# Inverse roots of twenty norms: from ScalarE's square root to bit operations and Newton steps on VectorE, in a two-layer MetaFormer kernel on Trainium2

## The chip, the cores and the metric

The kernel runs on one core of a Trainium2 chip. The metric is the device time of one execution in microseconds (us); a profile of one execution comes beside it. A core has a matrix engine (PE, with its weight loads counted apart as PEld), VectorE (DVE), ScalarE (ACT), GpSimd (POOL) and a queue engine (SP), which run their own instruction streams in order and wait for one another through semaphores.

## The reference

The input is `x`, four images of 384 channels and 32 x 32 positions, in fp32. There are two layers, and each has two residual steps, a mixing one and a feed-forward one, with a norm over the channels of one position ahead of each.

```python
def _ln_c(v, eps=1e-6):            # over the channels of a position
    m = jnp.mean(v, axis=1, keepdims=True)
    s = jnp.var(v, axis=1, keepdims=True)
    return (v - m) / jnp.sqrt(s + eps)
...
# --- layer 0 (metaformer) ---
x = x + _L0_conv_ref(_ln_c(x), ...)        # attention with relative tables, then w_proj
t = _to_tokens(x)
t = t + _L0_ffn_ref(_ln_t(t), ...)         # 384 -> 1536, exact Gelu, -> 384, weights are Kronecker products
x = _from_tokens(t, x)
# --- layer 1 (metaformer) ---
x = x + _L1_conv_ref(_ln_c(x), ...)        # sum of depthwise convolutions, folded into one of 7 x 7
t = _to_tokens(x)
t = t + _L1_ffn_ref(_ln_t(t), ...)         # softmax gate, top 2 of 4 experts, exact Gelu
x = _from_tokens(t, x)
```

`_ln_t` is the same over the last axis, with `eps=1e-5`. Four norms are taken of each image, then: one ahead of attention, and three behind it.

## The kernel before

The program has three phases. `qkv_phase` takes the first norm and makes queries, keys and values; `attention_phase` runs until about 1507 us; `rest_phase` does all the rest, and the change is in it alone.

In `rest_phase` an image is a tile `xb` of 128 partitions x 3 channel chunks x 1024 positions, worked on in two halves of 512 positions (`TOK`). The steps of an image b are these:

- `project` (L971): nine matmuls of a half (`proj_ps`), VectorE's addition of bias and residual (L980), and the statistics for the first norm behind attention.
- `net` (L988): the feed-forward of layer 0. The inverse root is spread over the partitions by `to_partitions` (L110): VectorE multiplies it into a diagonal (`s_dg`, L115) and PE multiplies ones with it (`all_ps`, L117). Twelve Gelus on ScalarE (`hs` from `f_ps`, L1022) stand between two sets of matmuls; VectorE adds the result to `xb` (L1030).
- `normalise` (L1051): statistics of the second norm, mean and inverse root each through `to_partitions`, then VectorE subtracts the mean (`xc`, L1061).
- `image` (L1065): VectorE multiplies by the scale into a padded image `img`. `convolve` (L1079): bias (L1084) and then 49 taps of three chunks, each one VectorE instruction of 128 x 1024 (L1089); in image 0 a part of the taps is done on PE by diagonal matmuls (`tap_ps`, `taps_ps`).
- `gates` (L1184): logits by PE (`gate_ps`, L661), statistics of the third norm (eight groups of 128 positions), `g_shift`, then `gate_weights` (L679) with a softmax, whose exponential is ScalarE's (L694), and the top two. The ranks of the chosen follow on PE (`before_ps`, L755) and VectorE.
- `scatter` (L1223): GpSimd writes the normalised rows to their slots in HBM.
- `blocks` (L1244): the experts, in blocks of 128 rows that are gathered again (`xg`), transposed (`xT_ps`), multiplied with weights that GpSimd fetches (`e_ps`, L1301), put through Gelu on ScalarE with a bias (`eh`, L1304) and multiplied again (`y_ps`, L1279). Four groups have 13, 16, 16 and 22 blocks; a block has twelve steps. `combine` adds the experts' results to `xb` at the end.

All three norms take their statistics in `token_stats` (L78): PE transposes 128 positions (`row_ps`, L87), VectorE takes mean and variance (`s_st`, `s_mv`, L89 and L90), and at the end ScalarE takes the root of the variance plus `eps` (L96) and VectorE its reciprocal (L97). It is called twice an image by `project`, twice by `normalise`, with 128 x 4 values each, and once by `gates` with 128 x 8 values: twenty calls. `row_ps`, `proj_ps`, `f_ps` and `e_ps` share the three PSUM banks of the pool `ps_h`.

The order of each engine's instructions comes from two places. The program interleaves generators: `blocks` calls `more` after every step of an expert block, and `more` (L1475) advances the work of the coming images (`others`, L1407) for as long as a clock of estimated costs says so; `convolve` yields such a cost per tap. The numbers that `token_stats` and the others yield are those estimates. Below that, a list scheduler with modelled times sets each engine's order; instructions that pass through `pin` or `keep_in_program_order` (the taps of images 0 and 1, and a one-column `memset` after each tap of images 1 to 3, L1097) keep theirs. The compiler puts a table load ahead of each activation on ScalarE whose function is not in the table that is loaded. Root, Gelu and Exp alternate behind attention.

Of the kernel before, what the change touches and what calls it, by code (L numbers as in the profile page):

```python
# [11 lines left out]
F32 = mybir.dt.float32  # L12
AF = mybir.ActivationFunctionType
ALU = mybir.AluOpType
# [4 lines left out]
P = 128  # L19
# [33 lines left out]
NOT_LAST = (2 * (B - 1) * N + NEXP * (BLK - 1)) // BLK - sum(COUNTS[:-1])  # L53
MAXB = B * N // BLK
OUTSIDE = 1e6


PACKS = [
# [12 lines left out]
def bcast(ap, dim, n):  # L71

    dims = [list(d) for d in ap.ap]
    dims[dim] = [0, n]
    return bass.AP(ap.tensor, ap.offset, dims)


def token_stats(nc, pools, ident, x, eps, rows=None, step=4):  # L78


    small, psum, tag = pools
    nj = x.shape[2] // P
    mv = small.tile([P, nj, 2], F32, tag=f"s_mv{nj}", name="s_mv")
    for j in range(nj):
        ps = psum.tile([P, TOK], F32, tag=tag, name="row_ps")
        for k in range(KC):
            nc.tensor.transpose(ps[:, k * P : (k + 1) * P], x[:, k, j * P : (j + 1) * P], ident)  # L87
        st = small.tile([P, 6], F32, tag="s_st", name="s_st")
        nc.vector.bn_stats(st, ps[:, :C])  # L89
        nc.vector.bn_aggr(mv[:, j, :], st)  # L90
        if rows is not None:
            nc.scalar.copy(rows[j], ps[:, :C])
        if j % step == step - 1:
            yield 0.7 * step, 0.45 * step
    rstd = small.tile([P, nj, 1], F32, tag=f"s_rstd{nj}", name="s_rstd")
    nc.scalar.activation(rstd, mv[:, :, 1:2], AF.Sqrt, bias=eps)  # L96
    nc.vector.reciprocal(rstd, rstd)  # L97
    return mv[:, :, 0:1], rstd
# [11 lines left out]
def to_partitions(nc, pools, ident, one, values):  # L110

    small, psum, tag = pools
    nj = values.shape[1]
    dg = small.tile([P, nj, P], F32, tag="s_dg", name="s_dg", bufs=1)
    nc.vector.tensor_tensor(dg, bcast(ident.unsqueeze(1), 1, nj), bcast(values, 2, P), ALU.mult)  # L115
    ps = psum.tile([P, TOK], F32, tag=tag, name="all_ps")
    nc.tensor.matmul(ps, one, dg.rearrange("p j n -> p (j n)"), start=True, stop=True)  # L117
    return ps
# [535 lines left out]
def gate_logits(nc, pools, ident, gw, x, logits):  # L654


    psum, hid = pools
    ps = psum.tile([P, TOK], F32, tag="m", name="gate_ps")
    for k in range(KC):
        for h in range(N // TOK):  # L660
            nc.tensor.matmul(  # L661
                ps[32 * h : 32 * h + 32, :], gw[:, k, :], x[:, k, h * TOK : (h + 1) * TOK],
                start=(k == 0), stop=(k == KC - 1),
            )
    lgs = []
    for h in range(N // TOK):
        lg = hid.tile([P, TOK], F32, tag="hs", name="logits", bufs=HS)
        nc.scalar.copy(lg[:32], ps[32 * h : 32 * h + 32])
        lgs.append(lg)
    yield 0.1, 3.0  # L670
    for j in range(N // P):
        n0 = j % (TOK // P) * P
        nc.tensor.transpose(
            logits[:, 32 * j : 32 * j + 32], lgs[j // (TOK // P)][:32, n0 : n0 + P], ident[:32, :32]
        )
    yield 0.1, 1.5
# [140 lines left out]
def block_list(nc, small, cst, group, parts, done):  # L817
# [51 lines left out]
    nc.vector.tensor_tensor(over, ks, bcast(turned[:, :, m:], 1, nb), ALU.is_ge)  # L869
    nc.vector.scalar_tensor_tensor(where, over, OUTSIDE, where, ALU.mult, ALU.add)  # L870
    nc.vector.tensor_scalar(where, where, slot[:, 0:1], cst["wrow"][:, 0:1], ALU.add, ALU.add)
# [9 lines left out]
    nc.vector.tensor_tensor(held[:, :2], expert[:, :2, :], group["before"], ALU.is_equal)  # L881
    nc.vector.scalar_tensor_tensor(row, bcast(held, 2, 2), OUTSIDE, row, ALU.mult, ALU.add)
    nc.vector.tensor_copy(group["row"], row)
# [10 lines left out]
def rest_phase(tc, cst, x, ao_d, ins, xs_d, y_d, x2_d, out):  # L894
# [7 lines left out]
    nc = tc.nc  # L902
    ident, one = cst["ident"], cst["one"]
    with ExitStack() as es:
# [5 lines left out]
        small = es.enter_context(tc.tile_pool(name="r_small", bufs=2))  # L910
# [3 lines left out]
        stp = (small, ps_h, "h")  # L914
# [56 lines left out]
        def project(xs, at):  # L971

            if True:
                for m in range(KC):
                    ps = ps_h.tile([P, TOK], F32, tag="h", name="proj_ps")
                    for k in range(KC):
                        nc.tensor.matmul(  # L977
                            ps, wproj[:, k, m * P : (m + 1) * P], at[:, k, :], start=(k == 0), stop=(k == KC - 1)
                        )
                    nc.vector.scalar_tensor_tensor(  # L980
                        xs[:, m, :], ps, bproj[:, m : m + 1], xs[:, m, :], ALU.add, ALU.add
                    )
                    yield 0.7, 2.7

                _, rstd = yield from token_stats(nc, stp, ident, xs, cst["eps5"])
                return rstd

        def net(b, xs, rstd):  # L988
# [62 lines left out]
        def normalise(xb, halves, which=range(2)):  # L1051

            for half in which:
                xs = xb[:, :, half * TOK : (half + 1) * TOK]
                mean, rstd = yield from token_stats(nc, stp, ident, xs, cst["eps6"])
                mps = to_partitions(nc, (small, ps_m, "m"), ident, one, mean)
                sps = to_partitions(nc, (small, ps_m, "m"), ident, one, rstd)
                scale_sb = work.tile([P, TOK], F32, tag="scale", name="scale")
                nc.scalar.copy(scale_sb, sps)
                xc = work.tile([P, KC, TOK], F32, tag="xc", name="xc")  # L1060
                nc.vector.tensor_tensor(xc, xs, bcast(mps.unsqueeze(1), 1, KC), ALU.subtract)  # L1061
                halves.append((xc, scale_sb))
                yield 3.0, 2.0
# [120 lines left out]
        def gates(b):  # L1184

            xb, im = xbs[b], images[b]
            rows = [new_row() for _ in range(nj)]
            logits = ps_m.tile([P, TOK], F32, tag="m", name="logits_ps")
            yield from gate_logits(nc, (ps_m, hid), ident, gw, xb, logits)
            mean, rstd = yield from token_stats(nc, stp, ident, xb, cst["eps5"], rows, 2)  # L1190
            shift = small.tile([P, nj, 1], F32, tag="g_shift", name="g_shift")
            nc.vector.scalar_tensor_tensor(shift, mean, -1.0, rstd, ALU.mult, ALU.mult)
            yield from gate_weights(nc, small, logits, gb, rstd, im["mask"], im["top"])
            for j, row in enumerate(rows):
                nc.scalar.activation(row, row, AF.Identity, bias=shift[:, j, :], scale=rstd[:, j, :])
                im["rows"].append(row)
                if b and j % 2:
                    yield 1.0, 0.0
            yield 0.0, 0.0

        def new_row():
            return hid.tile([P, C], F32, tag="rows", name="rows", bufs=16)
# [181 lines left out]
        def ahead(b, halves):  # L1384
            if b < B:
                yield from enter(b)
                yield from normalise(xbs[b], halves)
# [107 lines left out]
@with_exitstack  # L1495
def metaformer_kernel(ctx: ExitStack, tc: tile.TileContext, ins, out):
    nc = tc.nc
    cp = ctx.enter_context(tc.tile_pool(name="const", bufs=1))
    dram = ctx.enter_context(tc.tile_pool(name="scratch", bufs=1, space=DRAM))
    ident = cp.tile([P, P], F32, name="ident")  # L1500
    make_identity(nc, ident)
    one = cp.tile([P, P], F32, name="one")
    nc.vector.memset(one, 1.0)
    cst = {"ident": ident, "one": one}
    for name, v in (("eps5", 1e-5), ("eps6", 1e-6)):
        t = cp.tile([P, 1], F32, name=name)
        nc.vector.memset(t, v)
        cst[name] = t
    qk_d = dram.tile([2 * C, NT], F32, name="qk_d")
    v_d = dram.tile([HEADS, P, B * NBLK * VW], F32, name="v_d")  # L1510
    ao_d = [dram.tile([C, B, YT * IMG], F32, name=f"ao_d{i}") for i in range(2)]
    x2_d = dram.tile([C, NT], F32, name="x2_d")
    xs_d = dram.tile([NEXP * CAP, C], F32, name="xs_d")
    y_d = dram.tile([ALL * BLK, C], F32, name="y_d")

    with tc.tile_pool(name="held", bufs=1) as pool:
        held = [
            pool.tile([64 + HD, *n], F32, name=name)
            for name, n in (("kq", [NT]), ("kk", [B, N // 2]), ("tab", [SPAN, ZW]))
        ]  # L1520
        qkv_phase(tc, cst, ins["x"], ins["w_qkv"], qk_d, v_d, xs_d)
        attention_phase(tc, cst, held, ins["tabs"], ins["tv"], qk_d, v_d, ao_d, list(range(HEADS)))
    rest_phase(tc, cst, ins["x"], ao_d, ins, xs_d, y_d, x2_d, out)
# [71 lines left out]
```

## Time and profile before

| what | value |
|---|---|
| runs | 3082.57, 3087.72, 3088.3 us; median 3087.72 |
| the profiled execution | 3092.57 us, span 3090.6 us, TensorE clock 0.976 |
| `attention_phase` ends, about | 1507 us |
| image 0: first convolution tap | 1592.2 us |
| gate of image 0, 1, 3: statistics ready | 1747.05, 2003.04, 2506.63 us |
| last norm done, experts of the last groups and the sum left | from about 2530 us |
| VectorE: taps of 128 x 1024 (L1089) behind 1500 us | 490, mean 1277 ns |
| VectorE: diagonal of the inverse root (L115) | 16, mean 729 ns |
| VectorE: reciprocal of 128 x 4 (L97) behind 1500 us | 16, mean 172 ns |

A line of groups names the code line, the engine, the operation, output and inputs by the program's names, then the count, busy time, mean duration, and the idle time of the engine just ahead with what ended it. In a line of waits, `PE all_ps L117 <- DVE s_dg L115` means that PE stood before `all_ps` until VectorE had finished `s_dg`. Times are counted from the first instruction of the profiled execution.

### The profile page before, as it was taken

The page shows a single profiled execution, that of the slowest core. Times are in us where ns is not written, and L with a number is a line of the kernel's source. Part 1 is how long each engine was busy: PE and PEld are TensorE (multiplying, and loading weights), DVE is VectorE, ACT ScalarE, POOL GpSimd, SP SyncE. Part 2 cuts the span into 40 slices and gives each one's busy share as a digit, 9 for nine tenths or more (in the row PEclk, how much of TensorE's full clock was granted, in tenths as well). Part 3 has the DMA queues.
Part 4 walks back from the last instruction along what each step waited for, and adds up shares of the span by engine and source line. Part 5 has one row for each costly group of instructions (what it writes and reads, how often), then busy time and mean ns, then how long its engine had stood idle before and what let it go on. Part 6 is the DMA issues. An engine that isn't in the chain of part 4 may idle for free.

```text
span 3090.6 us, 63376 instructions
## 1 busy us (share of the span) xinstructions
PE 2929.9 (95%) x25391; PEld 2020.6 (65%) x25391; DVE 1956.6 (63%) x3575; ACT 1370.8 (44%) x2833; POOL 1170.7 (38%) x1132
## 2 busy tenths in 40 slices
PE   8997999999999999999899789999999989999996
PEld 4544676777677677776533347776577867777775
DVE  2226787878787877777568869999899640001101
ACT  1104666666767666666322232333342243233332
POOL 3223747473747473737400122252124231124412
PEclk9998999999999999999999879999999999999998
DMA  3796565656565656564500314734243065366742
GB/s 123 259 320 212 130 203 131 206 132 203 134 202 134 200 131 196 136 199 128 186 21 34 128 31 156 274 136 154 75 175 132 26 229 215 134 227 250 263 180 72
DMA packets 262791, 500.55 MB, mean 162 GB/s; under 512 B 134736, under 2 KB 186832, under 8 KB 254816
## 3 DMA queue, kind: packets, MB, share of 16 engines
q1 hardware_dynamic: 169168, 247.12, 26.0%
q0 software_dynamic: 43424, 227.84, 20.0%
q10 hardware_dynamic: 49904, 21.53, 3.6%
q8 instruction: 200, 3.28, 0.5%
q14 instruction: 95, 0.78, 0.1%
HBM read 543.58 MB, written 152.37 MB: 225 GB/s over the span
## 4 chain that ended last, share of the span: by engine, by line
PE 67%; DVE 13%; issue 11%; POOL 4%; DMA 3%; ACT 2%; another core or an unknown queue 0%; SPq 0%; POOLq 0%; DVEq 0%; ACTq 0%
PE e_ps L1301 12%; PE y_ps L1279 12%; DVE xb L1089 8%; PE t_ps L410 7%; PE av_ps L227 7%; PE sc_ps L227 7%; PE tabq_ps L227 5%; PE a_ps L420 3%; PE tv_ps L227 2%; PE proj_ps L977 2%; PE tabk_ps L227 1%; PE tap_ps L1137 1%; DVE extra L402 1%; PE f_ps L1012 1%; PE o_ps L1016 1%
## 5 line engine op out<-in xcount | busy, mean ns | idle before, releaser
L1301 PEld LDWEIGHTS e_ps<-xT,w 128*128 128x128 f32 x4824 | 656.5, 193 | 217.7 <-issue 14.6
L353 POOL TENSOR_TENSOR bias<-b,s 128x416 f32<-128x416 f32 (+24 forms) x656 | 659.2, 1042 | 178.1 <-DMA s<-sd 157.5
L1301 PE MATMUL e_ps<-xT,w 128*128 128x128 f32 x4824 | 670.6, 277 | 14.1 <-DVE xb L1030 5.0
L1279 PE MATMUL y_ps<-w,eh 128*128 128x384 f32 x1608 | 651.9, 490 | 17.2 <-ACT eh L1304 14.8
L1089 DVE SCALAR_TENSOR_TENSOR xb<-img,pack,xb 128x1024 f32<-128x1024 f32 (+1 forms) x539 | 634.7, 1241 | 0.0
L1304 ACT ACTIVATE eh<-e_ps,w 128x128 f32<-128x128 f32 x804 | 292.9, 367 | 725.3 <-PE e_ps L1301 669.5
L1269 POOL DMA_INDIRECT w<-in_w,row x134 | 171.4, 1279 | 749.7 <-PE y_ps L1279 301.4
L402 DVE TENSOR_REDUCE extra<-arow 128x32 f32<-128x32 f32 (+24 forms) x768 | 381.3, 555 | 9.4 <-ACT arow L391 5.7
L381 DVE CUSTOM_DVE_ANT_0 arow<-sc_ps,bias 128x1024 f32<-128x1024 f32 x256 | 312.5, 1221 | 107.1 <-issue 55.5
L410 PEld LDWEIGHTS t_ps<-ident,arow 128*128 128x128 f32 x2048 | 221.2, 142 | 175.9 <-ACT aT L411 100.6
L391 ACT ACTIVATE arow<-arow,nm 128x1024 f32<-128x1024 f32 x256 | 302.4, 1181 | 70.8 <-DVE nm L381 70.8
L411 ACT COPY aT<-t_ps 128x512 f32<-128x512 f32 x512 | 278.6, 603 | 95.3 <-PE t_ps L410 95.0
L410 PE MATMUL t_ps<-ident,arow 128*128 128x128 f32 x2048 | 283.2, 282 | 17.1 <-ACT arow L391 17.0
L1282 DVE TENSOR_TENSOR yo<-y_ps,w 128x384 f32<-128x384 f32 x67 | 37.0, 553 | 396.0 <-PE y_ps L1279 387.8
L227 PE MATMUL sc_ps<-kk,qs 48*32 48x512 f32 x4096 | 279.2, 608 | 7.7 <-DVE nm L381 6.7
L1279 PEld LDWEIGHTS y_ps<-w,eh 128*128 128x128 f32 x1608 | 248.3, 193 | 31.9 <-ACT eh L1304 19.4
L227 PEld LDWEIGHTS av_ps<-aT,vb 128*64 128x64 f32 x4096 | 222.3, 137 | 52.0 <-ACT aT L411 40.4
L227 PE MATMUL av_ps<-aT,vb 128*64 128x128 f32 x4096 | 237.7, 274 | 0.0
L318 DVE STREAM_TRANSPOSE b<-tabk_ps 128x480 f32<-128x480 f32 x256 | 218.4, 983 | 23.5 <-PE tabk_ps L227 22.2
L227 PE MATMUL tabk_ps<-tab,kq 48*128 48x480 f32 x512 | 223.0, 582 | 6.1 <-DVE b L318 6.1
L227 PE MATMUL tabq_ps<-tab,kq 48*128 48x480 f32 x512 | 220.1, 579 | 2.1 <-ACT aT L411 1.4
L322 ACT COPY st<-tabq_ps 128x480 f32<-128x480 f32 x256 | 142.3, 560 | 71.0 <-PE tabk_ps L227 45.0
(211 smaller groups left out, 3163.4 us busy)
## 6 DMA issues: line engine op xcount, KB each, us to landing
sd<-st SPq DMA_DIRECT2D x128, 480.0 KB
s<-sd SPq DMA_DIRECT2D x256, 240.0 KB
xs_d<-zero POOLq DMA_DIRECT2D x8, 3072.0 KB
tvw<-in_tv SPq DMA_DIRECT2D x120, 192.0 KB
y_d<-yo SPq DMA_DIRECT2D x67, 192.0 KB
qk_d<-qk_sb POOLq DMA_DIRECT2D x48, 256.0 KB
qs<-qk_d SPq DMA_DIRECT2D x256, 48.0 KB
kq<-qk_d ACTq DMA_DIRECT2D x56, 192.0 KB
```

The costliest lines, as they stand in the source:

```text
L227: ins = nc.tensor.matmul(*args, **kw)
L318: turn = nc.vector.transpose(b2.rearrange("p e y x -> p x (e y)")[:, i + j], ps[:, j, : SPAN * IMG])
L353: nc.gpsimd.tensor_tensor(bias[:, y0:y1, :], bass.AP(b2.tensor, b2.offset + (e * IMG + y0) * IMG, [list(b2.ap[0]), [(step * IMG + 1) * IMG ...
L381: nc.vector.tensor_tensor_reduce(s["flat"], ps.rearrange("p h n -> p (h n)"), s["bias"].rearrange("p y x -> p (y x)"), -SCALE, BIG, ALU.ad ...
L391: nc.scalar.activation(s["flat"], s["flat"], AF.Exp, bias=s["nm"], scale=-1.0, accum_out=dn[:, y % YT : y % YT + 1])
L402: pin(nc.vector.tensor_reduce(ex[:, i, :], a[:, p0:p1, :].rearrange("p y x -> p x y"), AX.X, ALU.add))
L410: pin(nc.tensor.transpose(pt[:, j, :], s["flat"][:, k0 : k0 + P], ident))
L411: pin(nc.scalar.copy(aT[:, 4 * g : 4 * g + 4, s["y"] % YB, :], pt))
L1089: ins_ = nc.vector.scalar_tensor_tensor(acc[:, k, y0:y1], img[:, k, dy + y0 : dy + y1, dx : dx + IMG], w7[:, k, dy, dx : dx + 1], acc[:, k ...
L1279: nc.tensor.matmul(py, hs, w[:, o : o + C], start=(ff == 0), stop=(ff == NF - 1))
L1301: nc.tensor.matmul(ph, w[:, o : o + P], xT[k][:, c, :], start=(c == 0), stop=(c == KC - 1))
L1304: nc.scalar.activation(hs, ph, AF.Gelu, bias=w[:, o : o + 1])
```

## The change

In all twenty calls behind attention, `token_stats` adds `eps` on VectorE, takes the complement of the number's bits shifted right by one, reads that as a number, scales it by a constant (the guess of one over the root), and refines it by three Newton steps of three instructions each. The result replaces root and reciprocal. The constant column `eps5`, and the memset that filled it, go. `qkv_phase` keeps ScalarE's root.

```diff
+EPS5, EPS6 = 1e-5, 1e-6
+GUESS = 1.8352579511977553e-20
...
+def inverse_root(nc, small, v, eps):
+
+    U = mybir.dt.uint32
+    n = v.shape[1]
+
+    def new(name, dt=F32):
+        return small.tile([P, n, 1], dt, tag=f"i_{name}{n}", name=f"i_{name}")
+
+    x, bits, t = new("x"), new("bits", U), new("t")
+    y = small.tile([P, n, 1], F32, tag=f"s_rstd{n}", name="s_rstd")
+    nc.vector.tensor_scalar(x, v, eps, None, ALU.add)
+    nc.vector.tensor_scalar(bits, x.bitcast(U), 0xFFFFFFFF, 1, ALU.bitwise_xor, ALU.logical_shift_right)
+    nc.vector.tensor_scalar(y, bits.bitcast(F32), GUESS, None, ALU.mult)
+    for _ in range(3):
+        nc.vector.tensor_tensor(t, y, y, ALU.mult)
+        nc.vector.scalar_tensor_tensor(t, t, -0.5, x, ALU.mult, ALU.mult)
+        nc.vector.scalar_tensor_tensor(y, t, 1.5, y, ALU.add, ALU.mult)
+    return y
...
-def token_stats(nc, pools, ident, x, eps, rows=None, step=4):
+def token_stats(nc, pools, ident, x, eps, rows=None, step=4, bits=False):
...
+    if bits:
+        return mv[:, :, 0:1], inverse_root(nc, small, mv[:, :, 1:2], eps)
     rstd = small.tile([P, nj, 1], F32, tag=f"s_rstd{nj}", name="s_rstd")
     nc.scalar.activation(rstd, mv[:, :, 1:2], AF.Sqrt, bias=eps)
     nc.vector.reciprocal(rstd, rstd)
...
-                _, rstd = yield from token_stats(nc, stp, ident, xs, cst["eps5"])
+                _, rstd = yield from token_stats(nc, stp, ident, xs, EPS5, bits=True)
...
-                mean, rstd = yield from token_stats(nc, stp, ident, xs, cst["eps6"])
+                mean, rstd = yield from token_stats(nc, stp, ident, xs, EPS6, bits=True)
...
-            mean, rstd = yield from token_stats(nc, stp, ident, xb, cst["eps5"], rows, 2)
+            mean, rstd = yield from token_stats(nc, stp, ident, xb, EPS5, rows, 2, True)
...
-    for name, v in (("eps5", 1e-5), ("eps6", 1e-6)):
+    for name, v in (("eps6", EPS6),):
```

## The prediction

> **What bounds the kernel now.** I read the page first, for shares and the chain; then ScalarE's groups by form, which list the table loads; then what the matrix engine (PE) waits for, by stretch; then busy time by window; then timelines around the norms.
>
> ```profile
> PE 2929.9 (95%) x25391; PEld 2020.6 (65%) x25391; DVE 1956.6 (63%) x3575; ACT 1370.8 (44%) x2833; POOL 1170.7 (38%) x1132
> ...
> PE 67%; DVE 13%; issue 11%; POOL 4%; DMA 3%; ACT 2%; another core or an unknown queue 0%; SPq 0%; POOLq 0%; DVEq 0%; ACTq 0%
> ```
>
> The chain that ended last runs through PE and, for 13%, VectorE (DVE). ScalarE (ACT) has 2% of it: freeing it pays only where PE or VectorE stood waiting for it.
>
> ScalarE's groups from 1500 us to the end (count, busy us, mean ns, idle before):
>
> ```profile
> L96 ACT ACT_TABLE_LOAD x14 | 18.0, 1283 | 30.7 <-DVE s_mv L90 30.5
> L1304 ACT ACT_TABLE_LOAD x12 | 15.4, 1283 | 2.1 <-issue 1.9
> L1022 ACT ACT_TABLE_LOAD x4 | 5.1, 1283 | 5.0 <-PE f_ps L1012 5.0
> L694 ACT ACT_TABLE_LOAD x4 | 5.1, 1283 | 0.1
> L96 ACT ACTIVATE s_rstd<-s_mv,eps 128x4 f32<-128x4 f32 x16 | 4.8, 298 | 70.1 <-DVE s_mv L90 70.0
> ```
>
> 34 table loads, 43.6 us: 14 ahead of the roots, most others to get Gelu back. PE's waits, 1500 to 1850 and 1850 to 2530 (total us, times, longest):
>
> ```profile
> PE all_ps L117 <- DVE s_dg L115: 10.8, 6, 3.9
> ...
> PE gate_ps L661 <- DVE xb L1089: 7.4, 1, 7.4
> ...
> PE y_ps L1279 <- ACT eh L1304: 2.3, 2, 1.7
> PE f_ps L1012 <- ACT hs L1022: 1.9, 2, 1.2
> ```
>
> ```profile
> PE e_ps L1301 <- DVE xb L1030: 5.0, 2, 2.7
> PE y_ps L1279 <- ACT eh L1304: 4.7, 4, 2.0
> ```
>
> Early on PE waits for VectorE far more than for ScalarE; later both. After 2530 no norm is left. Busy us by window (PE, PEld, DVE, ACT, POOL):
>
> ```profile
> 1850.00:2000.00 150.00, 149.36 (x911) 116.35 (x910) 149.94 (x174) 45.25 (x121) 40.28 (x26) 1.00 0.53 200
> ...
> 2150.00:2214.00 64.00, 58.05 (x293) 29.56 (x291) 64.00 (x78) 26.68 (x54) 7.98 (x6) 1.00 0.04 13
> ...
> 2530.00:3090.00 560.00, 518.38 (x3118) 408.47 (x3117) 58.35 (x139) 163.45 (x428) 159.59 (x162) 0.97 0.54 195
> ```
>
> From 1850 to 2214 VectorE has next to no free time except around the gate (43.5 of 50 us busy from 2000 to 2050), so an instruction added there moves the convolution taps behind it.
>
> [...] The 1283 is in the trace[...]: at gate 1 the load of 2003.62 is followed by its root at 2004.92. I price a load at 1.30 us. [...] interleaved small instructions here start 0.08 to 0.09 us apart (2009.27, 2009.35, 2009.44). [...] Dependent steps are dearer here:
>
> ```profile
> 2008.47 0.19 DVE L697 TENSOR_REDUCE g_den<-g_pr 128x8 f32<-128x32 f32 x1 [2.04 <-ACT g_pr L694]
> 2008.69 0.20 DVE L698 RECIPROCAL g_den<-g_den 128x8 f32<-128x8 f32 x1
> 2008.93 0.19 DVE L699 TENSOR_TENSOR g_pr<-g_pr,g_den 128x32 f32<-128x32 f32 x1
> ```
>
> 0.22 to 0.24 us apart; I take 0.20 for 128x4 and 0.22 for 128x8. A chain of twelve alone is then 2.4 or 2.6 us; mixed with independent work it takes 12 x 0.09 = 1.1 us of VectorE.
>
> **The change part by part.** It removes 20 roots on ScalarE (0.30 us each), 20 reciprocals on VectorE (0.17 to 0.20) and the hop between the engines, and adds 240 VectorE instructions. In the compiled instruction order ScalarE's table loads behind attention go from 34 to 9: one Gelu at the start, then Exp and Gelu at each gate. PE and SP keep their order, POOL swaps a few neighbours, no DMA moves, no new wait between engines appears. The bitwise step has no row in the trace; its nearest, a 128x4 tensor_scalar, takes 0.16 us when undisturbed and 1.45 us once beside POOL. Hence 0.16; at worst 20 x 1.3 = 26 us of VectorE if every one were disturbed, at best nothing saved below 0.16. POOL is idle from 1550 to 1700, so I take 0.16.
>
> What twelve replace: with a load 2.45 us (gate 1, statistics ending 2003.04, next user 2005.49), without one 0.77 us (gate 0, 1747.05 to 1747.82). So a chain costs 1.65 where the root needed no load, nothing where it did.
>
> By stage, as shifts of the path that sets the end:
> - Image 0, net (1544): the Gelu load stood behind the root at 1542.11, hidden; now it waits for PE's first f_ps, exposed. 1.28 less 0.2 of slack: +1.1.
> - Image 0, normalise, half 0: the chain ends at 1565.75 by my count, where the reciprocal now ends at 1565.78: 0. Two loads (1563.9, 1565.5) go, but PE's 0.53 us wait there is for VectorE.
> - Image 0, half 1, and image 1, project (1583 to 1633): in the new order the chain's tail stands between the centring (1.75 us) and three bias instructions, so the diagonal of rstd goes from 1587.53 to about 1590.2 and the first convolution tap 2.5 later. PE catches up nothing, since its row_ps wait on VectorE's adds. The serial chain of image 1 adds 0.3: together +2.8.
> - Image 1, normalise (1704 to 1737): 0. VectorE has gaps of 1.22, 0.93 and 2.23 us here, and PE waits 7.4 at gate_ps for the convolution.
> - Gate 0 and image 2, project (1747 to 1773): +1.65 for a chain without a load, less the exposed Gelu load at 1771.51 (PE's 1.2 us wait on hs): +0.45. Running sum +4.35.
> - Image 2, normalise (1823 to 1842): three loads go, and PE's 0.57 and 1.71 us waits on eh. But the convolution of the next stretch starts when it did, and VectorE is full until gate 1: PE waits the 2.3 us back. 0.
> - Gate 1 (2003 to 2014): the chain equals what it replaces. Two loads go and PE's 1.19 us wait on eh with them, so the ranks come earlier: VectorE -1.65 (between 0 and -2.3).
> - Image 3, project (2100 to 2214): two chains among convolutions, VectorE full: 2 x 1.1 = +2.2. PE pays it in its two e_ps waits on L1030.
> - Gate 2 (2306): twelve instructions, each with a convolution tap between, come out some 19 us late; the ranks behind them had 23 us of slack. 0, or +1.1 if PE meets VectorE again before 2410.
> - Gate 3 (2506 to 2517): the root's load (2506.94) and the Gelu behind it (2508.56) make PE's 2.01 us wait on eh; the chain is no longer than before: -2.0 (-1 to -3.5).
> - After 2530: PE alone, nothing changed. 0.
>
> Sum: 1.1 + 2.8 + 0.45 - 1.65 + 2.2 - 2.0 = +2.9 us. The profiled execution took 3092.57 us (span 3090.6), 4.9 above the median of the runs shown, 3087.72. Against its own time that is 3095.5, against the median 3090.6: I say 3091.
>
> **The rivals.** *Faster:* everything PE lost to loads is collected: gate 0 -1.3, image 2 -2.3, gate 1 -2.3, gate 3 -3.5, with only the first +1.1 and image 3's +2.2 kept: about -6 to -8, 3080. For it: the y_ps waits on eh, 7.0 us, sit next to the loads. Against it: VectorE is full from 1850 to 2214 and takes back what PE gains.
>
> *Slower:* the serial chain where VectorE sets the pace. From 1507 to 1773 there are eleven norms in a part where PE waits on VectorE's diagonals (10.8 us in six waits) and on its taps. If each pays 1.65, less the 2.5 us of loads that PE sees there, that is 18 - 2.5 = +15.5; with image 3 and gate 2 in full (+3.3) and the gates' gain (-3.65), +15; if half of the early ones pay, +7. I put it at +11, 3099. For it: all_ps is the largest wait but one of that part. Against it: in six of the eleven a load goes whose time the chain just fills. It decides as soon as a chain delays a diagonal for which PE already waits by more than the 1.28 us of a load.
>
> *Not what it says:* loads that come back because Exp and Gelu still alternate. The compiled order keeps nine, so this can cost no more than now: 3088.
>
> **How the numbers follow.** Forecast 0.42 (its own range 3084 to 3097, from gate 1 at 0 or -2.3, gate 2 at +1.1, gate 3 at -1 to -3.5, and half of the +2.8 either way), faster rival 0.23 (3077 to 3083), slower rival 0.33 (3094 to 3106), no effect 0.02. 0.2% of 3088 is 6.2 us, about what these runs can tell from no change (they spread by 5.7). Faster by more: 0.19 + 0.01 = 0.20. Slower by more: 0.32 + 0.09 = 0.41. Between: 0.39. Leaving out about one in ten on each side, the range is 3080 to 3102.
>
> **What would show it.** Right: nine table loads behind 1500; PE's y_ps wait on eh in 1850 to 2530 down from 4.7 to about 2; the first tap of image 0 some 2.5 to 3.6 us later than 1592.2; hs wait near 1772 gone; e_ps waits on L1030 at 2214 longer than 5.0 in all. Wrong, to the fast side: the start of image 2's convolution (1842.5) not later than before. Wrong, to the slow side: all_ps waits in 1500 to 1850 above 18 us, or the start of 2530's PE-only part more than 7 us late.

## The result, and the profile after

| | before | after |
|---|---|---|
| median of six runs (lowest to highest), us | 3087.25 (3082.57 to 3088.3) | 3105.51 (3098.39 to 3113.76) |
| profiled execution / its span, us | 3092.57 / 3090.6 | 3102.78 / 3100.9 |
| TensorE clock of the profiled execution | 0.976 | 0.974 |

The change costs 18.3 us: the ratio of the times is 1.0062, 95% interval 1.0045 to 1.0079. The forecast of 3091 and its whole range, 3080 to 3102, lie below the measured median.

The page of the kernel after, busy time and the chain that ended last:

```profile
PE 2933.2 (95%) x25391; PEld 2019.7 (65%) x25391; DVE 1986.8 (64%) x3794; ACT 1333.9 (43%) x2788; POOL 1172.5 (38%) x1132
...
PE 70%; DVE 12%; issue 9%; DMA 3%; POOL 3%; ACT 2%; another core or an unknown queue 0%; SPq 0%; POOLq 0%; ACTq 0%; DVEq 0%
```

ScalarE has 37 us less work and VectorE 30 more, as intended. But the same 25391 matmuls keep PE as busy as before. (PE's share of the chain is 70% against 67%, but in other traces of the two kernels it is 66 to 70% as well, so nothing is read from it.) ScalarE's groups of the kernel after, from 1500 us on, show that the loads went:

```profile
L718 ACT ACT_TABLE_LOAD x4 | 5.1, 1283 | 0.1
L1328 ACT ACT_TABLE_LOAD x3 | 3.8, 1283 | 0.1
L1046 ACT ACT_TABLE_LOAD x2 | 2.6, 1283 | 5.1 <-PE f_ps L1036 5.0
```

Nine loads instead of 34. In both traces each of them, behind 1500 us, stands ahead of the first root, Gelu or Exp that follows another of the three. So the change does what it says. The chain of twelve costs what was priced, too. VectorE's groups of the kernel after, by form, from 1500 us on (count, busy us, mean ns, idle before):

```profile
L90 DVE TENSOR_SCALAR i_x<-s_mv 128x4 f32<-128x4 f32 x16 | 5.6, 349 | 0.2
...
L91 DVE TENSOR_SCALAR i_bits<-i_x 128x4 uint32<-128x4 uint32 x16 | 2.6, 165 | 0.1
```

The bitwise step takes 165 ns (0.16 was used). In the timeline of gate 3 the twelve steps start 0.20 us apart and end 2.43 us after the first, where the prediction used 0.22 and 2.6.

PE's waits of the kernel after, first from 1500 to 1850 us (total us, times, longest):

```profile
PE all_ps L141 <- DVE s_dg L139: 12.3, 7, 3.9
PE gate_ps L685 <- DVE xb L1113: 8.9, 1, 8.9
...
PE f_ps L1036 <- ACT hs L1046: 4.4, 2, 3.7
```

and from 1850 to 2530 us:

```profile
PE xT_ps L1287 <- DMA xg<-xs_d,slot: 4.8, 1, 4.8
PE e_ps L1325 <- DVE xb L1054: 3.8, 2, 2.1
PE e_ps L1325 <- DMA w<-in_w,row: 3.4, 1, 3.4
PE y_ps L1303 <- ACT eh L1328: 2.9, 3, 1.3
PE before_ps L779 <- DVE mask L733: 2.4, 2, 2.0
```

The wait for `s_dg` grew by only 1.5 us, so the serial chains are not where the 18 us are. The wait for `eh` fell from 4.7 to 2.9. Two waits are new in kind or size: 3.4 us for expert weights `w`, and 3.7 us for `hs`. What this table of waits can't show is PE working slower. For that I compared the times of like instructions in both traces, counted from the end of attention. Each entry is what a stretch lost against the trace of before; *again* and *third* are the changed kernel in two later series on two different chips, *control* is the kernel before on yet another chip. The stretch ahead of gate 1 ends with VectorE's last addition for an expert block there (`yo`), where VectorE is busy throughout; the other ends are Gelus, taps and expert blocks.

| stretch | predicted | after | third | again | control |
|---|---|---|---|---|---|
| to image 0's first Gelu | +1.1 | +2.0 | +1.1 | +1.7 | -0.9 |
| image 0's feed-forward | 0 | +5.9 | +0.1 | +5.9 | 0 |
| to the first tap | +2.5 | +2.5 | +2.5 | +2.7 | 0 |
| to image 2's first Gelu | +0.75 | -0.9 | +2.1 | +1.1 | +0.2 |
| image 2's feed-forward (L1046, Gelus 49 to 72) | 0 | +5.4 | +8.7 | -7.1 | +0.1 |
| to the last `yo` ahead of gate 1 | 0 | +0.1 | -0.4 | +0.2 | +0.6 |
| over gate 1 | -1.65 | +1.4 | +0.9 | +1.4 | 0 |
| image 3's project | +2.2 | +0.7 | +0.5 | +0.7 | +0.7 |
| over gate 2, to 2495 us | 0 | -0.7 | +2.1 | -0.8 | -2.0 |
| over gate 3, to 2580 us | -2.0 | +3.4 | +2.8 | -4.6 | -1.1 |
| to the end | 0 | -5.9 | -4.8 | -16.0 | -6.9 |

For *after* the column sums to +13.8; attention ended 3.6 us earlier in that trace, which makes the 10.2 by which the two profiled executions differ. The other 8 us of the 18.3 are the choice of executions: that of before lies 5.3 above its median, that of after 2.7 below. *Control* shows where executions can differ: unchanged, it is 6.9 shorter in the last stretch.

Most of what the prediction missed falls in four places: the feed-forwards of images 0 and 2, gate 1 and gate 3. In or just ahead of each, PE's clock is at half for a while. In all, behind attention, the traces have it at half for 117 us in before, 113 in the control, 141 in *after*, 135 in *third* and 116 in *again*. Half of the 24 us that *after* has more, 12 us, is an estimate of what that cost, against the 13.8 that the trace lost there; for *third* it is 9 us of 15.7. In image 0's feed-forward, PE's timeline before:

```profile
1569.63 1.13 PE L1012 MATMUL f_ps<-u,pack 32*128 32x512 f32 x6
1570.69 1.06 PE L1016 MATMUL o_ps<-hs,pack 128*32 128x512 f32 x6
```

and after:

```profile
1571.89 2.08 PE L1036 MATMUL f_ps<-u,pack 32*128 32x512 f32 x6
1573.91 1.93 PE L1040 MATMUL o_ps<-hs,pack 128*32 128x512 f32 x6
```

Six matmul records of the same shapes take nearly twice as long. Busy time by window (start and end, length, then PE, PEld, DVE, ACT and POOL with counts, PE's clock as a share of full speed, DMA share, GB/s) says it for the stretch, before and then after:

```profile
1559.00:1576.00 17.00, 16.47 (x68) 5.16 (x66) 8.14 (x14) 10.15 (x17) 0.00 (x0) 1.00 0.13 47
```

```profile
1559.00:1576.00 17.00, 17.00 (x40) 4.14 (x43) 8.85 (x24) 5.01 (x10) 0.00 (x0) 0.60 0.14 46
```

PE is busy for the whole window, yet gets through 40 matmuls instead of 68. PE's 97% against 100% would have told nothing; the count beside it and the clock do. In image 2's feed-forward, before and then after:

```profile
1774.00:1803.00 29.00, 25.43 (x71) 8.00 (x69) 16.55 (x25) 9.36 (x17) 15.92 (x16) 0.74 0.25 82
```

```profile
1774.00:1803.00 29.00, 22.59 (x56) 5.62 (x55) 14.02 (x40) 7.99 (x13) 19.67 (x20) 0.62 0.32 112
```

The clock was at 0.74 here before the change too, which the prediction's sum doesn't use.

### The profile page after: what moved, and what is told of

Read it like the earlier page. It is cut to its first block, busy times and chain, and to the rows that moved or that the text cites. A ratio compares the mean times of both kernels' runs of the same rounds, so it can differ in the third digit from the quotient of the medians.

```text
span 3100.9 us, 63559 instructions
## 1 busy us (share of the span) xinstructions
PE 2933.2 (95%) x25391; PEld 2019.7 (65%) x25391; DVE 1986.8 (64%) x3794; ACT 1333.9 (43%) x2788; POOL 1172.5 (38%) x1132
## 4 chain that ended last, share of the span: by engine, by line
PE 70%; DVE 12%; issue 9%; DMA 3%; POOL 3%; ACT 2%; another core or an unknown queue 0%; SPq 0%; POOLq 0%; ACTq 0%; DVEq 0%
PE e_ps L1325 13%; PE y_ps L1303 13%; PE t_ps L434 8%; PE av_ps L251 7%; PE sc_ps L251 7%; DVE xb L1113 6%; PE tabq_ps L251 6%; PE a_ps L444 3%; PE qk_ps L199 2%; PE tv_ps L251 2%; PE tabk_ps L251 1%; DVE extra L426 1%; PE tap_ps L1161 1%; PE v_ps L210 1%; DVE oT L503 1%
## 5 line engine op out<-in xcount | busy, mean ns | idle before, releaser
L1229 POOL DMA_INDIRECT xs_d<-rows,pos x64 | 75.2, 1175 | 274.1 <-DVE b_slot L875 240.1
```

## The experiments

They ran in five series, each on another chip (that of the first comparison is not on record), and the kernel before has another median in each: 3067.06, 3081.01, 3065.64, 3069.07 and 3086.03 us, against 3087.25 in the first comparison. A ratio is always against the kernel before on the same chip. "Lost" and "gained" in a stretch are against the trace of before, as in the table above; every run has one trace, of one execution, so these are single readings. The mean clock of a kernel is that over its runs.

### Series 1: which of the calls

*again* is the changed kernel without an edit. The others give calls their root on ScalarE back, in this way:

```diff
-                _, rstd = yield from token_stats(nc, stp, ident, xs, EPS5, bits=True)
+                _, rstd = yield from token_stats(nc, stp, ident, xs, cst["eps5"])
```

*only_project* keeps the change in the eight calls of `project`, *only_normalise* in the eight of `normalise`, *only_gates* in the four of `gates`.

> The changed kernel once more, to see which parts of its trace recur. Three theories of the +18 us. CLOCK: PE's granted clock falls to half in more places (in the first trace of the changed kernel from 1562 to 1576 us and from 1781 to 1805, 78 us of it between 1507 and 1850 against 61 before), and that is most of the time. SERIAL: the chains of twelve on VectorE where it sets the pace. GATES: the gains I counted at the gates did not come. CLOCK expects about +18 us again, with a half-rate stretch around 1562 or another in the same part, and times that follow the mean clock of each run (0.001 of clock is about 3 us). SERIAL expects the same shift at each norm in both traces (first tap of image 0 late by about 3.6 us net of clock), and no more than that.

> The four gates alone take the new root. CLOCK expects no difference beyond 3 us from the kernel before, since the feed-forward parts of images 0 and 1 are as before. SERIAL expects +1 to +3 (gate 0 has no load to save). GATES expects 0 to +4; my forecast's terms for the gates were +1.65, -1.65, 0 and -2.0, so -2.

> The eight norms ahead of the feed-forward alone take the new root. CLOCK expects a good part of the +18 (8 to 15 us), with half-rate stretches beside image 0's or image 2's feed-forward. SERIAL expects 8 of the 20 chains' share, +5 to +8. GATES expects +3, my forecast's terms for project.

> The eight norms ahead of the convolution alone take the new root. CLOCK expects +3 to +10, by whether a half-rate stretch falls beside image 0's second half. SERIAL expects +5 to +8. GATES expects +2.5, the one delay of image 0's second half that I counted.

| kernel | median, us | ratio (95%) | mean clock |
|---|---|---|---|
| before | 3067.06 | | .9778 |
| again | 3075.02 | 1.0025 (1.0014 to 1.0035) | .9757 |
| only_gates | 3066.39 | 1.0001 (0.9993 to 1.0009) | .9772 |
| only_project | 3071.41 | 1.0014 (1.0005 to 1.0023) | .9770 |
| only_normalise | 3076.02 | 1.0030 (1.0020 to 1.0040) | .9757 |

The same kernel that lost 18 us lost 8 here. `normalise` alone loses as much as the whole change, `gates` nothing. The parts don't add up: 4.4 for `project`, 9.0 for `normalise` and -0.7 for `gates` make 12.6, against 8.0. The loss comes with the clock: between runs of one and the same kernel of this series, 0.001 of clock goes with 2.4 us, so the 0.0021 that *again* has less stand for 5.0 of its 7.4 us (means), and 2.4 are left, near the +2.9 of the forecast's sum. That is a correlation. It doesn't say whether the lower clock makes the longer time or goes with something else that does, so the next series look at places.

### Series 2: image 0, and the length of the chain

*before_again* is the kernel before without an edit (the *control* above). *gelu_first* adds to the changed kernel a Gelu of one column ahead of image 0's statistics, so that the table is loaded early:

```diff
+        early = small.tile([P, 1], F32, tag="early", name="early")
+        nc.scalar.activation(early, at0[:, 0, :1], AF.Gelu)
         rstd0 = result(project(xs0, at0))
```

*image0_root* gives `project` and `normalise` of image 0 alone the root on ScalarE back; one of its four calls:

```diff
-        side = normalise(xbs[0], halves[0], (0,))
+        side = normalise(xbs[0], halves[0], (0,), False)
```

*one_step* makes one Newton step instead of three, so six instructions instead of twelve:

```diff
-    for _ in range(3):
+    for _ in range(1):
```

> The kernel before once more, for a trace beside those of the others of this call. In the parts run so far image 0's first tap came +10.3 us late in both traces of the changed kernel (counted from the end of attention), 5.9 of it in a half-rate stretch of PE's clock at the second half of the feed-forward (1562 to 1576). CLOCK expects no half-rate stretch there in this trace, and the first tap within 1.5 us of the first trace. SERIAL says nothing here.

> The changed kernel with one Gelu of a column ahead of image 0's projection, so that the table is there when the feed-forward begins: it takes away the exposed load, 1.3 us. CLOCK expects more than that if the clock then stays full in image 0's second half: 5 to 8 us less than the changed kernel, the first tap at +3 to +4. SERIAL expects -1.3 alone, the first tap at +9 if the half-rate stretch is there anyhow.

> Image 0's four norms of project and normalise keep ScalarE's root, the other sixteen take the new one. CLOCK expects image 0 as before (first tap within 1.5 us, no half-rate stretch at 1562) and a total at or below the kernel before, -5 to 0 us. SERIAL expects 16 of 20 chains to remain, so at least half of the changed kernel's excess, +4 or more.

> One Newton step instead of three: two steps of each norm are left out, so the roots are rougher and the chain has six instructions, 1.2 us shorter at 0.20 each. SERIAL expects each exposed chain to shrink by 1.2: the first tap of image 0 some 2.5 to 3.6 us earlier than with three steps, and 5 to 10 us less in all. CLOCK expects the half-rate stretch, if it is still there, to keep 5.9 of the +10.3, and a total within 4 us of the changed kernel.

*before_again* gave 3079.18 us in its one run. *gelu_first* took 3096.60 us, 1.0055 (1.0042 to 1.0068); *image0_root* 3093.55, 1.0044 (1.0031 to 1.0057); *one_step* 3087.67, 1.0023 (1.0014 to 1.0033).

With the load early, image 0's first Gelu came 0.2 us late instead of 1.1 to 2.0: this term of the forecast was real. What it is worth in the total can't be read, since the changed kernel itself didn't run on this chip. *image0_root* has all of image 0's delay gone (its first tap is 0.5 us early), and still 12.5 us of loss, where CLOCK expected -5 to 0; 6.0 us of its trace's loss are in image 2's feed-forward. So image 0 alone doesn't carry the loss on this chip. *one_step*, with half of the chain, lost 6.7 us where *gelu_first* lost 15.6; that fits SERIAL, but other things had changed in it as well (see the slower rival in the next section).

### Series 3: can matmuls keep the clock up?

The feed-forward's `f_ps` and `o_ps` are matmuls of 32 x 128 and 128 x 32, a quarter of the 128 x 128 of the largest in the trace (`e_ps`, `y_ps`). That a larger matmul among them would hold the clock up was my conjecture; no trace had shown it. The added one, ahead of each `f_ps`, writes what that overwrites:

```diff
+                        if b in (2,):
+                            nc.tensor.matmul(ph[:, :256], fold[:, 0, :], c1t[:, :2, :], start=True, stop=True)
```

*before_fill256* and *after_fill256* have it in image 2, *before_fill128* has half its columns, *after_fill02* has it in images 0 and 2.

> The kernel before with an added matmul of the whole array (128 x 128, 256 columns, its result overwritten) ahead of each first matmul of image 2's feed-forward. CLOCK: in all traces so far PE's clock is at half there (13.7 to 17.1 us in each of two halves) while PE is busy with matmuls that use a quarter of the array[...]: half-rate time between 1760 and 1820 under 15 us against 27 to 34, and -3 to +1 us in all, since 24 added matmuls of about 0.27 us cost up to 6.5. If the clock does not follow the array's use, the half-rate stretches stay and the kernel is 6 to 13 us slower.

> The same with 128 columns, 24 matmuls of about 0.14 us: up to 3.3 us at full clock. CLOCK expects less half-rate time than before but maybe not all of it gone: -6 to +1 us. Without a link, +3 to +7.

> The changed kernel with image 2's feed-forward filled by 256 columns. CLOCK expects the excess over the kernel before to fall by what image 2's half-rate time costs beyond the kernel before, to between +3 and +10 us, and less spread between its runs. Without a link, 6 us or more slower than the changed kernel (+14 or more).

> The same in images 0 and 2. CLOCK expects no half-rate stretch at 1562 to 1576 and the first tap of image 0 at about +8 instead of +10.3 (5.9 gained, 12 times 0.27 paid in the second half, and as much in the first, where PE does not stand still). Without a link, the first tap at +16 or more.

The medians were 3094.64 us (ratio 1.0090, 1.0067 to 1.0112), 3096.82 (1.0102, 1.0087 to 1.0116), 3088.94 (1.0076, 1.0063 to 1.0089) and 3108.55 (1.0130, 1.0114 to 1.0145). All four times miss what was expected of a link between array and clock, and the first two are longer than was expected without one. In *before_fill256* each half of image 2 took 17.5 us more, and the clock stayed at half for 30.7 us in each, while PE was busy for 64.4 of the 66 us from 1774 to 1840 (mean clock 0.61). In *after_fill256* the same matmuls ran at 0.92 there. In *after_fill02* the stretch in image 0 was gone, but twelve added matmuls of its first half cost 9 us at full clock, 0.75 each where 0.27 was expected (two `y_ps` of 384 columns, at 0.81 us, give that for 256), more than they could win. What these traces say: with more of the array in use the clock could still stay at half for 30.7 us, and nearly the same work ran at almost full clock in another kernel. They don't show that the array's use has no part in it. The kernel alone doesn't settle the form either: the six runs of *before_fill256* spread from 3081.16 us at a clock of 0.981 to 3108.42 at 0.972, on one chip, and its trace is of the second slowest.

### Series 4: image 0's and image 2's second norm

The two halves of `normalise` are two calls for each image. *only_norm0* changes image 0's two alone, *only_norm2* image 2's two; *no_norm02* changes the sixteen others, *no_normalise* the twelve of `project` and `gates`. The edit, here for *only_norm2* (there and in *only_norm0*, `project` and `gates` keep ScalarE's root):

```diff
-                mean, rstd = yield from token_stats(nc, stp, ident, xs, EPS6, bits=True)
+                mean, rstd = yield from token_stats(
+                    nc, stp, ident, xs, *((EPS6, None, 4, True) if any(xb is xbs.get(i) for i in (2,)) else (cst["eps6"],))
+                )
```

> The new root in image 0's two norms ahead of the convolution alone. In all traces so far where those two are changed (and the feed-forward is not filled) PE's clock is at half in the feed-forward's second half, at a cost of 3.3 to 5.9 us, and the first tap is 2.5 later still for the order of VectorE's work. If those belong to these two norms: first tap +5 to +8.5, a half-rate stretch between 1555 and 1580, +4 to +8 in all. If the clock there is chance, the first tap at +2.5 and no stretch.

> The new root in image 2's two norms ahead of the convolution alone. In all five traces where they are changed, with all three steps, PE runs 2.9 us ahead in the first blocks of experts, then waits 3.4 to 3.8 us for weights in one piece (in the others 0 to 0.6), the clock falls to half for 3.4 to 6.8 us directly after, and gate 1 comes 2.3 to 2.9 us later against VectorE than before. If these two norms do it: that wait, that stretch, gate 1 (gate_ps of image 1) +2.3 and +2 in all. My forecast's term for it was 0.

> The new root everywhere but in those four norms: sixteen norms. If the four carry the excess through waits and clock: no half-rate stretch between 1555 and 1580 or between 1900 and 1930, and within 3 us of the kernel before, or below it. If VectorE's chains as such carry it (SERIAL): more than half of the changed kernel's excess remains, +4 or more.

> The new root ahead of the feed-forward and at the gates only, twelve norms: project and gates alone gave +0.14% and 0.0% by their medians. If parts add up: 0 to +5 us. If it is the lost table loads at image 2's feed-forward that move its half-rate stretches, image 2's feed-forward is 4 to 8 us longer or shorter than before, by the stretch.

| kernel | median, us | ratio (95%) | mean clock |
|---|---|---|---|
| before | 3069.07 | | .9777 |
| only_norm0 | 3071.55 | 1.0009 (1.0000 to 1.0019) | .9777 |
| only_norm2 | 3070.56 | 1.0010 (1.0003 to 1.0017) | .9767 |
| no_norm02 | 3067.82 | 1.0003 (0.9992 to 1.0013) | .9779 |
| no_normalise | 3071.38 | 1.0000 (0.9987 to 1.0014) | .9779 |

*only_norm2* is the clean case: two calls changed, and one thing follows from another. PE's waits of *only_norm2* from 1780 to 2006 us begin with:

```profile
PE e_ps L1327 <- DMA w<-in_w,row: 4.1, 1, 4.1
```

In before the largest wait for these weights in that stretch is 0.6 us. PE's timeline, before and then *only_norm2* (in brackets the idle time ahead and what ended it):

```profile
1910.28 2.27 PE L1301 MATMUL e_ps<-xT,w 128*128 128x128 f32 x18 [0.60 <-DMA w<-in_w,row]
```

```profile
1904.93 3.70 PE L1327 MATMUL e_ps<-xT,w 128*128 128x128 f32 x18 [4.14 <-DMA w<-in_w,row]
```

and POOL's, which fetches the weights, before and then *only_norm2*:

```profile
1898.25 1.80 POOL L1269 DMA_INDIRECT w<-in_w,row  x1 [3.48 <-DVE yo L1282]
```

```profile
1891.90 1.80 POOL L1295 DMA_INDIRECT w<-in_w,row  x1 [5.86 <-DVE yo L1308]
```

The fetch goes into a buffer that the block before the last reads until VectorE has added its bias (`yo`), and `yo` stands among the convolution's taps in VectorE's order. Counted from the first `e_ps` of the group, `yo` ends at 67.6 us in before and at 67.8 in *only_norm2*. Without the table loads PE runs 2.3 us ahead of before on this count (2.9 in *after*), and then stands 4.1 us in one piece; in before it stood 0.6 us there, and 1.1 us more for `eh` at the start of the group. After the stand the same eighteen matmuls take 3.70 us instead of 2.27: the clock is at half for 3.4 us. PE comes late to gate 1, and the stretch over the gate loses 2.4 us; *only_gates*, where the gate's own loads go, gains 1.2 there. The sum of the two, +1.2, is near what the whole change lost over gate 1 (+1.4, +0.9, +1.4). This wait of 3.4 to 4.1 us is in every trace with that norm changed and three Newton steps (after, again, third, *only_normalise*, *gelu_first*, *image0_root*, *only_norm2*, the two *after_fill*), and is at most 1.8 us in the other eleven. In all nine, half clock sets in within 1.2 us of the wait's end; of the eleven, one has such a stretch there (*before_fill256*, behind a wait of 1.8). By the medians *only_norm2* costs 1.5 us in all.

*only_norm0* shows the other predicted delay by itself: the second half's chain puts the first tap 2.7 us later than the feed-forward (no such delay in *no_norm02* and *no_normalise*). But the half-rate stretch in image 0's feed-forward, which I had put down to that norm, is in *no_norm02* and *no_normalise* too, with 5.8 us each: that theory fell. (*one_step*, which the expectation passes over, had that norm changed and no such stretch.)

The changed kernel itself didn't run on this chip, so what the last two kernels of the table would have to save here isn't known.

### Series 5: does it hold on another chip?

*after_third* is the changed kernel, *no_norm02_more* the same code as *no_norm02*.

> The changed kernel a third time, beside the next on one chip. CLOCK with the two norms: slower than the kernel before by 5 to 18 us, the wait for weights of 3.4 us or more and the half-rate stretch behind it, and gate 1 late by more than 2 us against VectorE.

> The sixteen norms without images 0's and 2's ahead of the convolution, on the same chip as the changed kernel: within 3 us of the kernel before and 5 us or more under the changed kernel, if those four carry the excess; within 3 us of the changed kernel if they don't.

Before took 3086.03 us here (mean clock .9765), *after_third* 3104.86, 1.0064 (1.0046 to 1.0081; clock .9725), *no_norm02_more* 3100.72, 1.0045 (1.0026 to 1.0063; clock .9740). The first comparison repeats itself on this chip; that the kernel without those four norms is as fast as before does not. By the medians they account for 4 of 19 us here, and the two intervals overlap.

What differs most between these traces is in image 2's feed-forward. Its first half (Gelus 49 to 60) takes 15 us at half clock in before. *again* needs 12.0 for it and *no_norm02* 9.5; the same code needs 23.6 in *after*, 23.6 in *after_third* and 24.1 in *no_norm02_more*. Busy time by window of *no_norm02*, to be held against the two lines of before and after:

```profile
1774.00:1803.00 29.00, 24.83 (x90) 9.49 (x90) 24.96 (x60) 11.73 (x20) 22.13 (x21) 0.96 0.33 114
```

90 matmuls at a clock of 0.96, where before had 71 at 0.74 and after 56 at 0.62. PE's timeline in *after_third*:

```profile
1783.53 4.21 PE L1036 MATMUL f_ps<-u,pack 32*128 32x512 f32 x4
1790.71 2.07 PE L1036 MATMUL f_ps<-u,pack 32*128 32x512 f32 x2 [2.98 <-ACT hs L1046]
```

and ScalarE's:

```profile
1785.02 0.60 ACT L1046 ACTIVATE hs<-f_ps 128x512 f32<-128x512 f32 x1 [2.26 <-PE o_ps L1040]
1790.06 0.60 ACT L1046 ACTIVATE hs<-f_ps 128x512 f32<-128x512 f32 x1 [4.45 <-remote]
1794.98 0.60 ACT L1046 ACTIVATE hs<-f_ps 128x512 f32<-128x512 f32 x1 [4.32 <-PE o_ps L1040]
```

PE and ScalarE hand each other one Gelu at a time, each standing while the other works: PE stands 3.0 us for `hs`, ScalarE 4.45 and 4.32 us. In the trace of *again* PE's longest wait for `hs` in this place is 0.7 us. "remote" means that the profile shows no releaser in this core's streams, so what holds ScalarE the first time can't be read from it.

Is the form of this stretch the chip's, or one execution's? One trace of each can't tell. The trace of *again* is of its second fastest execution (3069.23 us at a clock of 0.978; its median is 3075.02, its mean clock 0.9757), *only_norm0* changes nothing in image 2 and needs 9.5 us there too, and *before_fill256* showed how far executions of one kernel on one chip can lie apart.

No kernel here beats both: *only_gates*, *no_normalise* and *no_norm02* stand at the time of before on the chips of series 1 and 4.

## Why the prediction was wrong

Its direction was open (0.41 for slower, 0.39 for no difference), its time 14.5 us too low, and its range ended 3.5 us short. By its own steps:

- **Removed and added work: right.** Nine loads, twelve steps at the pitch that was used. (Gate 0's +1.65 takes its chain at 2.4 us, though the prediction's own price for 128x8 was 2.6; gate 3's measures 2.43.) Image 0's exposed Gelu load (+1.1; +1.1 to +2.0) and the order's delay of the first tap (+2.5; +2.5 to +2.7) came as said, and *gelu_first* and *only_norm0* each show one of them alone. Gate 2 cost nothing beyond what the unchanged kernel differs by in two traces. Image 1's `normalise` has no stretch of its own in the table; its stretch lost -0.9 to +2.1, where +0.75 was forecast.
- **Image 3, project, +2.2: too much.** +0.5 to +0.7, which the control has as well. The e_ps waits that were to grow shrank, from 5.0 to 3.8 us.
- **"Image 0, normalise, half 0 ... 0": failed in two of three traces of the changed kernel.** The chain's end was right. The matmuls next to it ran at half clock for 13.7 us, which cost 5.9. Of the 12 traced kernels with something of image 0 changed and no matmuls added there, nine have such a stretch; of the seven with nothing changed there, one has, a short one. In *after* and *again* PE was busy, as the profile counts it, all through and for over 10 us ahead of it (in *after* 11.40 of 11.40 us), so it follows on no stand of PE, and what set it off is open.
- **"Image 2, normalise ... PE waits the 2.3 us back. 0": right that it waits it back, wrong that this is free.** *only_norm2* shows it. PE gives the time back in one wait of 3.4 to 4.1 us for weights whose buffer VectorE frees, and then works at half clock (3.4 us of it in *only_norm2*, 6.8 in *after*). That turns gate 1 from a gain of 1.2 (forecast -1.65) into a loss of 0.9 to 1.4.
- **"Gate 0 and image 2, project ... Running sum +4.35": the sum ended where the largest loss begins.** Image 2's feed-forward lost 5.4 us in *after* and 8.7 in *after_third*, and gained 7.1 in *again*. The tell "hs wait near 1772 gone" came out the other way: the waits for `hs` from 1500 to 1850 grew from 1.9 to 4.4 us. That the same code does both speaks against a fixed price of the added instructions, and for the state in which PE and ScalarE meet. What decides on that state, and whether it goes with the chip or with the single execution, is open.
- **Gate 3, -2.0: failed in *after* and *third*.** The wait for `eh` of 2.01 us ahead of the ranks is gone, as said. PE stands for the ranks as long as before. Behind them it stood for `eh` in before too, 3.1 us in three waits of up to 1.6; now it is 4.1 us in two. The ranks in before, then the ranks and the two waits in *after*:

```profile
2513.91 0.41 PE L755 MATMUL before_ps<-mask,pack 128*128 128x32 f32 x2 [2.06 <-DVE mask L709]
```

```profile
2527.10 0.41 PE L779 MATMUL before_ps<-mask,pack 128*128 128x32 f32 x2 [2.04 <-DVE mask L733]
...
2529.08 1.65 PE L1303 MATMUL y_ps<-w,eh 128*128 128x384 f32 x2 [1.35 <-ACT eh L1328]
...
2547.50 0.91 PE L1303 MATMUL y_ps<-w,eh 128*128 128x384 f32 x2 [2.76 <-ACT eh L1328]
```

So the waits for `eh` around this gate fell from 5.1 us to 4.1 only. The `y_ps` at 2529.08 take 1.65 us, where they take 0.81 at full clock a few us earlier; the clock is at half for 6.8 us there, and for 3.4 more behind the third line, against 3.4 in all in before. Over the gate *after* lost 3.4 and *after_third* 2.8, where the control gained 1.1. *again* gained 4.6, but that says nothing of the gate: *only_norm2*, whose gates are unchanged, gained 4.8.

Two of the prediction's signs tell the same: image 0's first tap came at 1599.0 us, 6.8 later than 1592.2 instead of 2.5 to 3.6, and the part that begins at 2530 in before came 16 us late, where more than 7 was to show the slow side.

The term that failed is therefore one that the sum didn't have: PE's clock. The page of before shows it, in the row of PE's clock by slices and in the 0.74 of one window; the sum took every matmul at the length of its row. Behind attention the half-rate stretches of before and *after* last 3.4 us or a multiple of it (3.4, 6.8, 10.2, 13.7 and, once in *after*, 23.9), but for the last, which the end of the kernel closes (31.4 and 31.8). In *only_norm2* one comes with a stand of 4.1 us. In image 0 none follows on a stand: the stretch of *after* that is 17.00 of 17.00 us busy has a clock of 0.60, so PE, busy as the profile counts it, did not have its full clock there. What makes the clock fall isn't shown by these traces.

The slower rival (3094 to 3106) holds the time of the first comparison, by another way than its own. It wanted the diagonals late; the wait for `s_dg` grew 1.5 us, and stayed far below its mark of 18. *one_step* speaks against it in part only: on one chip it lost 6.7 us where *gelu_first* with full chains lost 15.6, but its weights' wait had shrunk to 1.5 us and its stretch in image 0 was gone as well, so chain length and clock aren't told apart by it.

**Shown:** the exposed load, the order's delay, and the chain from image 2's norm over the weights' wait to gate 1, a small part of the loss (1.5 us by itself). **Seen, cause open:** the half-rate stretch in image 0, and the long or short form of image 2's feed-forward, the largest single difference between the traces of *after* and *again* ahead of the last stretch (12.5 us).

## What to carry to other kernels

In this kernel, where PE is busy for 95% of the span, what the change adds and removes summed to +2.9 us, and it cost 18.3: among other things short stands of PE became one of 3.4 to 4.1 us, with the clock at half behind it (for 3.4 us in *only_norm2*). So put a line for the clock into the sum: mark where it already is below full in the profile of before, and where an engine that gets faster will meet a buffer that another engine frees. And before trusting a few tenths of a per cent, measure on a second chip, and trace more than one execution: this change cost 0.25% in one series, and 0.62 and 0.64% in two others.

## What the hardware showed beside

- **An addition of four columns took 3.08 us.** VectorE's timeline of the kernel after, and then POOL's of the same time:

```profile
1527.63 3.08 DVE L90 TENSOR_SCALAR i_x<-s_mv 128x4 f32<-128x4 f32 x1
1530.74 0.17 DVE L91 TENSOR_SCALAR i_bits<-i_x 128x4 uint32<-128x4 uint32 x1
```

```profile
1519.83 10.85 POOL L1143 TENSOR_TENSOR w<-half,pack 128x3136 f32<-128x3136 f32 x2 [1.38 <-issue]
```

It ends as POOL's work ends, as it does in *again* and *after_third*, where it took 3.07 and 3.51 us; it makes the mean of 349 ns in the group above. (The prediction took its price from POOL's idle time, which begins at 1550.) No run tried it without POOL's work.
- **Six small matmuls took as long as two that had a larger one ahead.** The matmuls of three `f_ps` (six records of 32 x 128, in different rows by the program) take 1.13 us together at full clock. In *after_fill02*, with a matmul of 128 x 256 ahead of each, the two records of one `f_ps` take 1.12 us by themselves, and the added matmul's two records 0.70. For each of the twelve the first half of image 0 came 0.75 us later.
- **Chips differ.** The same kernel before took 3065.6 to 3086.0 us (medians) on five chips, a wider range than the 18.3 us that the change cost.
